# Filler products and a ScalarE softmax in the last attention steps of a gated graph network

## The chip, the cores and the metric

The kernel runs on one NeuronCore of a Trainium2 chip. The core has TensorE (matrix products, PE in the profile, with its weight loads as PEld), VectorE (DVE), ScalarE (ACT), GpSimd (POOL) and SyncE (SP), which starts the transfers. Each engine works through its own list of instructions in the order in which the program has them; engines wait for each other by semaphores. The metric is the device time of one execution in microseconds, the median of several runs. For the kernel before it is 2128.97 us (three runs, 2126.75 to 2130.69). The profile is one further execution, with a span of 2129.0 us from first to last instruction.

## The reference

There are 128 graphs of 128 nodes with 256 features, in float32. Layer 0 normalises and runs three rounds of a gated graph network; layer 1 is one attention step over each graph's edges. Cut to what is computed:

```python
# layer 0
h = relu(layernorm(x))
for i in range(3):
    m = h @ weight[i]
    aggr = einsum('bst,bsd->btd', A, m)          # A = adj != 0
    h = gru_cell(aggr, h, w_ih, w_hh, b_ih, b_hh)
x = x + h
# layer 1
h = relu(layernorm(x))
Wh = h @ W
s = Wh.sum(-1)
e = leaky_relu(s[:, :, None] + s[:, None, :], 0.2)
e = where(adj == 0, -inf, e)
x = x + softmax(e) @ Wh
```

## The kernel before

**Tiling.** The 128 graphs are cut into 32 groups of four (`G = 4`, `NG = 32`). A group goes through three gated rounds, `gru` for the first two and `gru_rows` for the third (which leaves the result with nodes on partitions in `x1`), and then through `attention`. The gate products of a round are fixed chains of float32 products into six banks of the accumulator memory (`x_rz`, `x_n`, `y_rz`, `y_n`, `q_rz`, `q_n`); two more banks, `misc`, serve everything else. The list `turns` says in which order the rounds of the groups take the gate banks, so that rounds of three groups lie interleaved. At the end groups 29, 30 and 31 remain, and the last entry is round 2 of group 31.

**What sets the order.** No engine's order is written out by hand. Every piece of work is recorded with `op(engine, ns, fn, reads, writes, ...)`: its engine, a price in ns, what it reads and writes, and a due time. `Plan.run` then lists all of them. It walks a model clock for each engine, takes of the pieces that are ready the one that can start first, and among equals the one with the lowest rank; the rank is the due time less all that must follow. Gate products are bound to a fixed order among themselves. Only the order that comes out goes into the program; the prices do not. An engine whose next instruction waits, waits, even where the one behind it could start. A buffer of kind `turn`, such as the gate banks, goes to its users in the order of their `phase`.

**The attention step.** Group 31 does it in two halves of two graphs (`lo`, `hi`), the others in one piece. For a group of four:

- `normed` (L488 to L504): statistics of `x1` on VectorE (`st`, `mv`), the reciprocal root on GpSimd (`rs`), `nm` on VectorE, and the normalised `h1` on ScalarE. There is one `h1` buffer, so the next group's waits until this group's products have read it.
- L899: four sums on VectorE give `s`; L917 puts the mask into `e`.
- L923: TensorE turns `s` into a row (`misc`); L929 and L930 add both on VectorE, L932 is the leaky slope, L934 the row maximum `top`, L936 `low`, the bias of the exponential.
- L941: ScalarE computes the exponentials; L943 and L944 their sums `den` and the reciprocals `rden`, on VectorE.
- For the last two groups TensorE turns `e` (L953) and ScalarE copies it to `eT` (L955); earlier groups do this by a transfer. L619 multiplies with `h1` in two halves `k`, each copied to `uT` by ScalarE (L624).
- L966 multiplies with the layer's weights ("rows product" in what follows, two graphs at a time), L971 scales by `rden` and adds to `x1` on VectorE, L974 stores.

Ahead of everything, L309 multiplies the identity `ident` (128 x 128, float32) with itself eight times[...].

Of the kernel before, what the change touches and what calls it, by code (L numbers as in the profile page):

```python
# [13 lines left out]
OP = mybir.AluOpType  # L14
# [5 lines left out]
ALPHA = 0.2  # L20
SETS = 4
EARLY = 3
SLOT = 18150
MARGIN = 8000
GATES = 18150
# [11 lines left out]
class Plan:  # L37
# [25 lines left out]
        uses.append(b)  # L63
        return b

    def op(self, eng, ns, fn, reads=(), writes=(), room=(), due=None, mark=None,
           turn=None, two=False, lag=None):

        i, deps = len(self.nodes), set()
        for b in room:
            if b.prev is not None:
                deps.update(a[0] for a in b.prev.accesses)
        for is_write, group in ((False, reads), (True, writes)):
            for item in group:
                b, lo, hi = item if isinstance(item, tuple) else (item, 0, 1 << 30)
                for j, w, l, h in b.accesses:
                    if (w or is_write) and l < hi and lo < h:  # L80
                        deps.add(j)
                if is_write and b.prev is not None:
                    deps.update(a[0] for a in b.prev.accesses)
        for is_write, group in ((False, reads), (True, writes)):
            for item in group:
                b, lo, hi = item if isinstance(item, tuple) else (item, 0, 1 << 30)
                b.accesses.append((i, is_write, lo, hi))
        deps.discard(i)
        bufs = {id(x[0] if isinstance(x, tuple) else x): (x[0] if isinstance(x, tuple) else x)
                for x in list(reads) + list(writes) + list(room)}  # L90
        free = [b for b in bufs.values() if self.tags[b.tag][1] in ("free", "turn")]
        for b in free:
            b.users.append(i)
            b.left += 1
        self.nodes.append([eng, ns, fn, deps, free, self.due if due is None else due,
                           two or eng == "POOL", self.LAG[eng] if lag is None else lag])
        if due is not None:
            self.chain.append(i)
        if mark is not None:
            self.marks[mark] = i  # L100
        if turn is not None:
            self.turns.append((i, turn))
# [108 lines left out]
def kernel(  # L211
# [79 lines left out]
    def ap(b):  # L291
        return phys[(b.tag,) + b.slot]
# [187 lines left out]
        to_sbuf("ACT", D, ps, W["w1_sum"], 0)  # L480


    def normed(src, dst, lo=0, hi=G):

        st, mv, rs, nm = buf("st"), buf("mv"), buf("rs"), buf("nm")
        part = slice(lo, hi)
        for b in range(lo, hi):
            op("DVE", 415, lambda b=b: nc.vector.bn_stats(ap(st)[:, b, :], ap(src)[:, b, :]),  # L488
               [(src, b, b + 1)], [(st, b, b + 1)])

        def aggr():
            for b in range(lo, hi):
                nc.vector.bn_aggr(ap(mv)[:, b, :], ap(st)[:, b, :])
        op("DVE", 160 * (hi - lo), aggr, [st], [mv])

        def rstd():
            nc.gpsimd.tensor_tensor(ap(rs)[:, part], ap(mv)[:, part, 1], eps[:, part], OP.add)
            nc.gpsimd.tensor_tensor(ap(rs)[:, part], ap(rs)[:, part], neghalf[:, part], OP.pow)
        op("POOL", 1300, rstd, [mv], [rs])
        op("DVE", 170, lambda: nc.vector.scalar_tensor_tensor(  # L500
            ap(nm)[:, part], ap(mv)[:, part, 0], -1.0, ap(rs)[:, part], op0=OP.mult, op1=OP.mult),
           [mv, rs], [nm])
        for b in range(lo, hi):
            op("ACT", 520, lambda b=b: nc.scalar.activation(  # L504
                ap(dst)[:, b, :], ap(src)[:, b, :], AF.Relu, bias=ap(nm)[:, b:b + 1],
                scale=ap(rs)[:, b:b + 1]), [(src, b, b + 1), rs, nm], [(dst, b, b + 1)])
# [384 lines left out]
    def attention(g, a, x1, h1, lo, hi):  # L891

        part, n = slice(lo, hi), hi - lo
        w1, w1_sum = W["w1"], W["w1_sum"]
        normed(x1, h1, lo, hi)
        s = buf("s")
        for b in range(lo, hi):
            hw = buf("hw")
            op("DVE", 520, lambda b=b, hw=hw: nc.vector.scalar_tensor_tensor(  # L899
                ap(hw), ap(h1)[:, b, :], 1.0, ap(w1_sum), op0=OP.mult, op1=OP.mult,  # L900
                accum_out=ap(s)[:, b:b + 1]), [(h1, b, b + 1), w1_sum], [hw, (s, b, b + 1)],
               two=True)

        e, top, low, den, rden = (buf(t) for t in ("e", "top", "low", "den", "rden"))

        def wide(t):
            return ap(t)[:, part, None].to_broadcast([P, n, N])

        def es():
            return ap(e)[:, part]

        def small(t):
            return ap(t)[:, part]
        cost = 155 + 134 * n
        op("DVE", 150 + 66 * n, lambda: nc.vector.tensor_scalar(  # L917
            es(), ap(a)[:, part], 0.0, -BIG, op0=OP.is_equal, op1=OP.mult), [(a, lo, hi)], [e])
        s_all = buf("misc")

        def turn_s():
            for b in range(lo, hi):
                nc.tensor.transpose(flat(s_all)[:, b * N:(b + 1) * N],  # L923
                                    ap(s)[:, b:b + 1].to_broadcast([P, P]), ident)

        def spread():
            return flat(s_all)[:, lo * N:hi * N].rearrange("p (b n) -> p b n", n=N)
        op("PE", 110 * n, turn_s, [s], [s_all], [e])
        op("DVE", cost, lambda: nc.vector.tensor_tensor(es(), es(), spread(), OP.add), [s_all], [e])  # L929
        op("DVE", cost, lambda: nc.vector.tensor_tensor(es(), es(), wide(s), OP.add), [s], [e],  # L930
           two=True)
        op("DVE", cost, lambda: nc.vector.scalar_tensor_tensor(  # L932
            es(), es(), ALPHA, es(), op0=OP.mult, op1=OP.max), [], [e], two=True)
        op("DVE", cost, lambda: nc.vector.tensor_reduce(small(top), es(), AX.X, OP.max),  # L934
           [e], [top])
        op("DVE", 150, lambda: nc.vector.tensor_scalar(  # L936
            small(low), small(top), -BIG / 1e3, -1.0, op0=OP.max, op1=OP.mult), [top], [low])

        def exps():
            for b in range(lo, hi):  # L940
                nc.scalar.activation(ap(e)[:, b, :], ap(e)[:, b, :], AF.Exp, bias=ap(low)[:, b:b + 1])  # L941
        op("ACT", 320 * n, exps, [low], [e], turn=(g + 2, 1, "rz"))
        op("DVE", cost, lambda: nc.vector.tensor_reduce(small(den), es(), AX.X, OP.add), [e], [den])  # L943
        op("DVE", 170, lambda: nc.vector.reciprocal(small(rden), small(den)), [den], [rden])  # L944
        eT, uT = buf("eT"), buf("uT")
        if g < NG - 2:
            turned_weights(e, eT)
        else:
            p_e = buf("misc")

            def turn():
                for b in range(lo, hi):
                    nc.tensor.transpose(flat(p_e)[:, b * N:(b + 1) * N], ap(e)[:, b, :], ident)  # L953
            op("PE", 110 * n, turn, [e], [p_e], [eT])
            op("ACT", 190 + 100 * n, lambda: nc.scalar.copy(  # L955
                ap(eT)[:, part].rearrange("p b n -> p (b n)"), flat(p_e)[:, lo * N:hi * N]),
               [p_e], [(eT, lo, hi)])

        weighted(h1, eT, uT, lo, hi)
        for m in range(lo, hi, 2):  # L960
            ps = buf("misc")

            def rows_product(m=m, ps=ps):
                for b in range(2):
                    for k in range(KD):
                        nc.tensor.matmul(ap(ps)[:, b, :], ap(uT)[:, k, (m + b) * N:(m + b + 1) * N],  # L966
                                         ap(w1)[:, k, :], start=(k == 0), stop=(k == KD - 1))
            op("PE", 4 * 432, rows_product,
               [(uT, m // 2, m // 2 + 1), (uT, 2 + m // 2, 3 + m // 2), w1], [ps])
            for b in range(2):  # L970
                op("DVE", 480, lambda b=b, i=m + b, ps=ps: nc.vector.scalar_tensor_tensor(  # L971
                    ap(x1)[:, i, :], ap(ps)[:, b, :], ap(rden)[:, i:i + 1], ap(x1)[:, i, :],
                    op0=OP.mult, op1=OP.add), [ps, rden], [(x1, m + b, m + b + 1)])
        op("SP", 100, lambda: nc.sync.dma_start(  # L974
            out[g * G + lo:g * G + hi].rearrange("b n d -> n b d"), ap(x1)[:, part]),
           [(x1, lo, hi)], [])
# [49 lines left out]
```

## Time and profile before

| what | value |
|---|---|
| time, median of 3 | 2128.97 us |
| span of the profiled run | 2129.0 us, mean granted TensorE clock 0.994 |
| TensorE busy | 2108.4 us |
| VectorE busy | 1701.3 us |
| ScalarE busy | 1536.5 us |
| GpSimd busy | 923.8 us |
| last gate product leaves TensorE | 2090.67 us |
| last rows product (L966) leaves TensorE | 2124.94 us |

A row of the profile's groups or of its list in order of time has the line in the code, the engine, the operation, `out<-in` by the names of the buffers, the shape, and how many instructions of this kind follow each other (`x8`); the start and the duration in us stand ahead of it in the list in order of time. A note in brackets gives the idle time before it and what ended it. A float32 product of the code can be more than one row of the trace. Matmuls are pipelined, so the recorded duration of one is longer than the distance to the next; for what a product costs, take the distance. The granted clock says at which share of its full clock TensorE was let run in a stretch.

### The profile page before, as it was taken

What the parts mean: (1) busy time and instruction counts of PE and PEld (TensorE: products, weight loads), DVE (VectorE), ACT (ScalarE), POOL (GpSimd) and SP (SyncE); (2) the same over time, 40 slices, a digit from 0 to 9 for tenths busy, and PEclk for the clock granted to TensorE, in tenths of its full rate; (3) what the DMA queues carried; (4) which work ended last, traced back from release to release, by engine and by line L of the source; (5) the groups of instructions that cost most, each with busy time, mean ns of one, the idle gap of its engine ahead of it and who ended that gap; (6) DMA issues with size and microseconds to landing.
All of it is one profiled execution on the core that took longest, in us unless ns stands there. A gap on an engine that the chain in (4) does not pass through costs nothing. (4 is left out here: it accounts for less than half of the span.)

```text
span 2129.0 us, 34073 instructions
## 1 busy us (share of the span) xinstructions
PE 2108.4 (99%) x12550; PEld 1882.8 (88%) x12550; DVE 1701.3 (80%) x3364; ACT 1536.5 (72%) x2771; POOL 923.8 (43%) x889
## 2 busy tenths in 40 slices
PE   8999999999999999999999999999999999999997
PEld 7888888898888998889998898998889988898896
DVE  7767898778787887877888787887878887877785
ACT  5567787767777676877767777677776777676663
POOL 5544454344543435434444443444434454434331
PEclk9999999999999999999999999999999999999997
DMA  4222223232222322323222322222223222212220
GB/s 144 45 50 50 48 51 72 50 65 54 64 67 55 79 56 50 68 58 80 45 60 58 75 67 50 65 56 64 66 55 75 60 50 70 60 31 53 58 75 30
DMA packets 333430, 129.35 MB, mean 61 GB/s; under 512 B 264656, under 2 KB 333008, under 8 KB 333264
## 3 DMA queue, kind: packets, MB, share of 16 engines
q1 hardware_dynamic: 333264, 127.18, 26.3%
q8 instruction: 98, 1.61, 0.3%
q14 instruction: 68, 0.56, 0.1%
HBM read 45.36 MB, written 16.78 MB: 29 GB/s over the span
## 5 line engine op out<-in xcount | busy, mean ns | idle before, releaser
L702 ACT COPY t_rz<-y_rz 128x512 f32<-128x512 f32 x192 | 112.3, 585 | 188.8 <-PE y_rz L663 114.3
L565 POOL TENSOR_TENSOR r<-rows 128x512 f32<-128x512 f32 x128 | 140.4, 1117 | 229.8 <-ACT rows L548 99.9
L712 DVE TENSOR_TENSOR t_rz<-t_rz,q_rz 128x512 f32<-128x512 f32 x192 | 131.3, 684 | 88.0 <-PE q_rz L663 40.4
L633 POOL TENSOR_TENSOR hs<-hT 128x512 f32<-128x512 f32 x96 | 131.8, 1373 | 156.3 <-PE y_n L670 72.4
L663 PE MATMUL y_rz<-hs,s_hh 128*128 128x256 f32 x768 | 197.4, 379 | 0.3 <-ACT t_rz L702 0.3
L663 PE MATMUL y_rz<-gs,s_x 128*128 128x256 f32 x768 | 197.1, 379 | 0.0
L663 PEld LDWEIGHTS y_rz<-gs,s_x 128*128 128x128 f32 x768 | 145.9, 190 | 19.8
L637 POOL TENSOR_TENSOR hs<-hT,hs 128x256 f32<-128x256 f32 x96 | 77.0, 802 | 198.1 <-PE q_n L670 160.4
L663 PEld LDWEIGHTS y_rz<-hs,s_hh 128*128 128x128 f32 x768 | 144.0, 190 | 20.1 <-issue 1.0
L590 POOL TENSOR_TENSOR pl<-d,pl 128x512 bf16<-128x512 f32 x64 | 80.8, 1264 | 185.1 <-ACT pl L588 184.9
L568 POOL TENSOR_TENSOR p<-r 128x512 bf16<-128x512 f32 x128 | 159.6, 1267 | 0.0
L712 DVE TENSOR_TENSOR t_n<-t_n,q_n 128x512 f32<-128x512 f32 x192 | 131.3, 684 | 26.4 <-PE q_n L670 12.6
L585 POOL TENSOR_TENSOR d<-hT,pl 128x512 f32<-128x512 f32 x64 | 77.6, 1214 | 139.2 <-DVE hT L791 65.2
L608 ACT COPY aT<-misc 128x512 f32<-128x512 f32 x192 | 112.0, 585 | 27.1 <-PE misc L605 23.3
L663 PE MATMUL x_rz<-hT,s_hh 128*128 128x256 f32 x512 | 131.5, 379 | 0.0
L663 PE MATMUL x_rz<-aT,s_x 128*128 128x256 f32 x512 | 131.4, 379 | 0.0
L966 PE MATMUL misc<-w,uT 128*128 128x256 f32 x512 | 125.5, 390 | 0.8 <-ACT uT L624 0.7
L829 POOL TENSOR_TENSOR x<-x,u 128x512 f32<-128x512 f32 x64 | 82.5, 1305 | 100.1 <-DMA x<-in_x_dram 54.9
L785 DVE TENSOR_TENSOR d<-hT,u 128x512 f32<-128x512 f32 x128 | 115.4, 901 | 10.5 <-ACT u L782 10.5
L663 PE MATMUL y_n<-hs,s_hh 128*128 128x256 f32 x384 | 114.3, 379 | 0.0
L663 PE MATMUL y_n<-gs,s_x 128*128 128x256 f32 x384 | 114.3, 379 | 0.0
L966 PEld LDWEIGHTS misc<-w,uT 128*128 128x128 f32 x512 | 98.6, 196 | 15.6 <-ACT uT L624 2.1
(219 smaller groups left out, 6418.5 us busy)
## 6 DMA issues: line engine op xcount, KB each, us to landing
rows<-in_x_dram SPq DMA_DIRECT2D x32, 512.0 KB, 4.2
x<-in_x_dram SPq DMA_DIRECT2D x32, 512.0 KB, 4.0
out_dram<-x SPq DMA_DIRECT2D x31, 512.0 KB, 2.9
at<-in_adj_dram SPq DMA_DIRECT2D x32, 256.0 KB, 2.8
plT<-pl SPq DMA_TRANSPOSE x186, 3.3
rz<-in_L_gnn_w_ih_dram SPq DMA_DIRECT2D x1, 768.0 KB, 5.0
rz<-in_L_gnn_w_hh_dram SPq DMA_DIRECT2D x1, 768.0 KB, 7.7
e<-in_L_gnn_weight_dram SPq DMA_DIRECT2D x3, 256.0 KB, 7.8
```

What stands on the lines that cost most here:

```text
L565: op("POOL", 1106, lambda part=part: nc.gpsimd.tensor_tensor(ap(r1)[:, part], ap(rows)[:, part], top(rows)[:, part], OP.subtract), [(rows, ...
L568: op("POOL", 1050, lambda part=part: nc.gpsimd.tensor_tensor(ap(p3)[:, part], ap(r1)[:, part], top(r1)[:, part], OP.subtract), [(r1, n, n ...
L585: op("POOL", 1150, lambda k=k, r=r: nc.gpsimd.tensor_tensor(ap(r), ap(hT)[:, k], part(pl, k, 0), OP.subtract), [(hT, 2 * k, 2 * k + 2), (p ...
L590: op("POOL", 1150, lambda k=k, r=r: nc.gpsimd.tensor_tensor(part(pl, k, 2), ap(r), part(pl, k, 1), OP.subtract), [r], [(pl, k, k + 1)])
L608: op("ACT", 590, lambda k=k, ps=ps: nc.scalar.copy(ap(dst)[:, k, :], flat(ps)), [ps], [(dst, 2 * k, 2 * k + 2)])
L633: op(eng, cost, lambda: sub(ap(w)[:, 0:2, :], blocks()[:, 1::2, :], blocks()[:, 0:2, :], OP.subtract), [t], [(w, 0, 2)], two=True)
L663: nc.tensor.matmul(ap(bank)[:, half, :], ap(w)[:, i - 1, q, :], source(t, sums), start=(first and c == 0 and m == 0), stop=False, skip_gro ...
L702: op("ACT", 590, lambda: nc.scalar.copy(ap(t), ap(y)), [y], [t], mark=mark)
L712: op("DVE", 690, lambda: nc.vector.tensor_tensor(ap(t), ap(t), ap(q), OP.add), [q], [t])
L785: op("DVE", 690, lambda j=j, d=d, cols=cols: nc.vector.tensor_tensor(ap(d), ap(hT)[:, j, :], ap(u)[:, cols], OP.subtract), [(hT, lo, hi), ...
L829: op("POOL", 1290, lambda cols=cols, part=part: nc.gpsimd.tensor_tensor(part(x1), part(x1), ap(u)[:, cols], OP.add), [(u, lo, hi)], [(x1, ...
L966: nc.tensor.matmul(ap(ps)[:, b, :], ap(uT)[:, k, (m + b) * N:(m + b + 1) * N], ap(w1)[:, k, :], start=(k == 0), stop=(k == KD - 1))
```

## The change

It has two parts, both at the end of the run.

The first adds filler products on TensorE in the attention steps of groups 30 and 31. `warm(t, ns)` records a piece of TensorE work that reads `t` (so that it can't stand before `t` is there), multiplies a slice of `t` with the identity and then the identity with itself `ns // 110` times. All of it goes into the bank `x_n`, as a use of that bank after the last gates, and nothing reads the result. The pieces carry `late=True`, a due time behind all other work. They are for TensorE's clock, so that it stays up in the stretches in which TensorE waits for the softmax.

The second applies to groups 29, 30 and 31 (`ENDING = 3`). The addition of `s` and the leaky slope (L930 and L932) become one ScalarE instruction per graph, a Prelu with `s` as its bias, and the sums of the exponentials (L943) become the accumulator output of the exponentials themselves. This is for VectorE, which is then free of three operations per group.

The line numbers of the changed kernel are higher: L619 becomes L650, L923 becomes L956, L941 becomes L984, L953 becomes L999, L966 becomes L1012 and L971 becomes L1017; the fillers are L500 (the read of `t`) and L502 (identity with identity).

```diff
+ENDING = 3
...
     def op(self, eng, ns, fn, reads=(), writes=(), room=(), due=None, mark=None, late=False,
            turn=None, two=False, lag=None):
...
-        self.nodes.append([eng, ns, fn, deps, free, self.due if due is None else due,
+        self.nodes.append([eng, ns, fn, deps, free, 10 ** 9 if late else self.due if due is None else due,
                            two or eng == "POOL", self.LAG[eng] if lag is None else lag])
...
+    def warm(t, ns, get=None):
+        if plan.group < NG - 2:
+            return
+        if not after_gates:
+            phase_now, plan.phase = plan.phase, len(turns)
+            after_gates.append(buf("x_n"))
+            plan.phase = phase_now
+        b = after_gates[0]
+
+        def products():
+            here = flat(b)
+            what = get() if get else plain(t)[:, :P]
+            cols = what.shape[1]
+            nc.tensor.matmul(here[:, :cols], ident, what, start=False, stop=False, skip_group_check=True)
+            for _ in range(ns // 110):
+                nc.tensor.matmul(here[:, :P], ident, ident, start=False, stop=False,
+                                 skip_group_check=True)
+        op("PE", 60 + ns, products, [t, b], [], late=True)
...
     def normed(src, dst, lo=0, hi=G):
...
+            if dst is not src:
+                warm((st, b, b + 1), 330, lambda b=b: ap(st)[:, b, :])
...
+        if dst is not src:
+            warm(mv, 1100, lambda: ap(mv)[:, lo, :])
...
+        if dst is not src:
+            warm(nm, 440, lambda: ap(nm)[:, part])
...
     def attention(g, a, x1, h1, lo, hi):
...
+        ending = g >= NG - ENDING
...
+            warm((h1, b, b + 1), 440, lambda b=b: ap(h1)[:, b, :P])
...
-        op("DVE", cost, lambda: nc.vector.tensor_tensor(es(), es(), wide(s), OP.add), [s], [e],
-           two=True)
-        op("DVE", cost, lambda: nc.vector.scalar_tensor_tensor(
-            es(), es(), ALPHA, es(), op0=OP.mult, op1=OP.max), [], [e], two=True)
+        def leaky():
+            for b in range(lo, hi):
+                nc.scalar.activation(ap(e)[:, b, :], ap(e)[:, b, :], AF.Prelu, bias=ap(s)[:, b:b + 1],
+                                     alpha=ALPHA)
+        if ending:
+            op("ACT", 320 * n, leaky, [s], [e])
+        else:
+            ...
...
+        warm(top, 110, lambda: small(top))
...
+        warm(low, 330 * n, lambda: small(low))
...
                 nc.scalar.activation(ap(e)[:, b, :], ap(e)[:, b, :], AF.Exp, bias=ap(low)[:, b:b + 1],
+                                     **(dict(accum_out=ap(den)[:, b:b + 1]) if ending else {}))
-        op("ACT", 320 * n, exps, [low], [e], turn=(g + 2, 1, "rz"))
-        op("DVE", cost, lambda: nc.vector.tensor_reduce(small(den), es(), AX.X, OP.add), [e], [den])
+        op("ACT", (400 if ending else 320) * n, exps, [low],
+           [e, den] if ending else [e], turn=(g + 2, 1, "rz"))
+        if not ending:
+            op("DVE", cost, lambda: nc.vector.tensor_reduce(small(den), es(), AX.X, OP.add), [e], [den])
```

More of the change, by code (lines that the diff above doesn't have):

```diff
@@ L64, in buf, with op @@
         return b
-    def op(self, eng, ns, fn, reads=(), writes=(), room=(), due=None, mark=None,
+    def op(self, eng, ns, fn, reads=(), writes=(), room=(), due=None, mark=None, late=False,
            turn=None, two=False, lag=None):
@@ L480, in weights @@
         to_sbuf("ACT", D, ps, W["w1_sum"], 0)
+    def warm(t, ns, get=None):
[15 more added lines that the diff above has]
+        op("PE", 60 + ns, products, [t, b], [], late=True)
+    after_gates = []
     def normed(src, dst, lo=0, hi=G):
@@ L929, in attention @@
         op("DVE", cost, lambda: nc.vector.tensor_tensor(es(), es(), spread(), OP.add), [s_all], [e])
-        op("DVE", cost, lambda: nc.vector.tensor_tensor(es(), es(), wide(s), OP.add), [s], [e],
-           two=True)
-        op("DVE", cost, lambda: nc.vector.scalar_tensor_tensor(
-            es(), es(), ALPHA, es(), op0=OP.mult, op1=OP.max), [], [e], two=True)
+        def leaky():
[5 more added lines that the diff above has]
+        else:
+            op("DVE", cost, lambda: nc.vector.tensor_tensor(es(), es(), wide(s), OP.add), [s], [e],
+               two=True)
+            op("DVE", cost, lambda: nc.vector.scalar_tensor_tensor(
+                es(), es(), ALPHA, es(), op0=OP.mult, op1=OP.max), [], [e], two=True)
         op("DVE", cost, lambda: nc.vector.tensor_reduce(small(top), es(), AX.X, OP.max),
            [e], [top])
+        warm(top, 110, lambda: small(top))
         op("DVE", 150, lambda: nc.vector.tensor_scalar(
             small(low), small(top), -BIG / 1e3, -1.0, op0=OP.max, op1=OP.mult), [top], [low])
+        warm(low, 330 * n, lambda: small(low))
         def exps():
             for b in range(lo, hi):
-                nc.scalar.activation(ap(e)[:, b, :], ap(e)[:, b, :], AF.Exp, bias=ap(low)[:, b:b + 1])
-        op("ACT", 320 * n, exps, [low], [e], turn=(g + 2, 1, "rz"))
-        op("DVE", cost, lambda: nc.vector.tensor_reduce(small(den), es(), AX.X, OP.add), [e], [den])
+                nc.scalar.activation(ap(e)[:, b, :], ap(e)[:, b, :], AF.Exp, bias=ap(low)[:, b:b + 1],
+                                     **(dict(accum_out=ap(den)[:, b:b + 1]) if ending else {}))
[3 more added lines that the diff above has]
+            op("DVE", cost, lambda: nc.vector.tensor_reduce(small(den), es(), AX.X, OP.add), [e], [den])
         op("DVE", 170, lambda: nc.vector.reciprocal(small(rden), small(den)), [den], [rden])
```

## The prediction

> **What bounds the kernel now.** I read the page's busy shares first, then TensorE by windows of time, then its waits, then the chain that ended last, and last the list in order of time from 2070 us on.
>
> From the busy shares: TensorE is the wall, and no other engine is near it.
>
> ```profile
> PE 2108.4 (99%) x12550; PEld 1882.8 (88%) x12550; DVE 1701.3 (80%) x3364; ACT 1536.5 (72%) x2771; POOL 923.8 (43%) x889
> ```
>
> TensorE's waits from 60 to 2090 us sum to 2.2 us. So the body cannot gain more than 2.2 us, and whatever the change wins or loses comes after 2090.67 us, where the last gate product leaves the array. The same engine by windows there (columns: stretch, length, busy time of PE, weight loads, DVE, ACT, POOL, granted clock, DMA):
>
> ```profile
> 2093.50:2096.90 3.40, 0.90 (x5) 0.45 (x3) 3.40 (x7) 1.36 (x4) 1.57 (x1) 0.98 0.00 0
> 2096.90:2100.30 3.40, 2.57 (x11) 2.20 (x12) 3.30 (x8) 1.13 (x3) 0.00 (x0) 0.50 0.00 0
> ...
> 2107.10:2110.55 3.45, 3.45 (x10) 2.71 (x9) 1.65 (x6) 0.00 (x0) 0.00 (x0) 0.52 0.00 0
> 2110.55:2113.90 3.35, 1.15 (x7) 0.56 (x5) 2.48 (x7) 0.36 (x2) 0.00 (x0) 0.99 0.00 0
> 2113.90:2117.30 3.40, 2.85 (x11) 2.44 (x12) 2.77 (x9) 1.67 (x6) 0.00 (x0) 0.50 0.16 57
> ```
>
> The clock column halves after a stretch with 0.90 us of TensorE work, and returns after one that is full. This is what the fillers are for. What the halving costs is seen in the list in order of time, with the same eight products at full and at half clock:
>
> ```profile
> 2078.07 1.06 PE L619 MATMUL misc<-eT,h 128*128 128x128 f32 x8
> 2090.78 3.62 PE L966 MATMUL misc<-w,uT 128*128 128x256 f32 x16
> 2098.82 2.08 PE L619 MATMUL misc<-eT,h 128*128 128x128 f32 x8 [0.68 <-ACT eT L955]
> 2104.32 6.72 PE L966 MATMUL misc<-w,uT 128*128 128x256 f32 x16 [0.68 <-ACT uT L624]
> ```
>
> The chain that ended last shows the end: TensorE's last products, two adds, the store.
>
> ```profile
> 2117.76 3.42 PE misc L966 x8
> ...
> 2123.36 1.58 PE misc L966 x6
> 2124.94 0.02 issue
> 2124.97 0.48 DVE x L971
> ```
>
> Last, the price of a filler. A filler is a float32 product of the identity with itself, and the kernel already has eight of exactly this form at its start (L309, two loops of four). The trace has 16 rows for them:
>
> ```profile
> L309 PE MATMUL y_rz<-ident x8: 421/421/581, 1.4 to 3.0; 128*128 128x128 f32 x8
> L309 PE MATMUL y_n<-ident x8: 274/421/421, 3.2 to 4.6; 128*128 128x128 f32 x8
> ```
>
> So each `matmul(ident, ident)` in the code is two products in the trace. A transpose (L923, L953) is one row for one.
>
> [...]0.50 and 1.00 alternate at about 2096.9, 2110.5, 2113.9 and 2120.7 us, all multiples of 3.4 us apart, and 2.57 us busy of 3.40 were not enough to return. [...]a 128-column float32 product takes two rows of 0.111 us (L619: 8 rows from 2077.97 to 2078.86 us of weight loads), one in bf16 (L605) starts every 0.055 us, so 0.222 against 0.055. [...]the trace has one load, of 1.28 us, for Tanh, Exp, Relu and copies together.
>
> **The change part by part.** The new order of instructions on each engine is the built program's own; it is fixed, and an engine takes its list from the top.
>
> *Slope and sums on ScalarE, groups 29 to 31.* Removes from VectorE L930, L932 and L943: 3 x 0.69 us for a group of four graphs, 3 x 0.42 for each half of the last group. Adds to ScalarE one Prelu per graph, nearest row L941 (0.32 us apart in a row of four), and an accumulator on Exp; before has no such row, so between 0.08 us (VectorE's accumulator read in L899)[...]; I take the first. Prelu could need another table set: [...]I take 0, since five functions share the one load. Neither end matters: ScalarE is 9.60 us busy in the 34.27 us from 2090.67 to 2124.94 us, and the walk below leaves it waiting for TensorE. Value on the path: 0.
>
> *Fillers.* They may write only `x_n`'s bank, in a phase after the last gates, so all of them stand behind the last gate product: none delays a gate. But from there they stand between the real products. The planner prices a filler at 110 ns (`ns // 110`); it takes 0.222 us at full clock. The planner put them where it saw holes of its own size, and TensorE cannot skip them. Walking TensorE's new list from 2090.67 us (t = 0), at full clock:
>
> ```
>  t end  what stands there
>   4.4   4 x (h1 read + 4 fillers), 1.11 each
>   7.9   group 29 rows product, 16 rows x 0.2206   (before: at 0 to 3.5)
>  10.7   low + 12 fillers (2.8)
>  11.2   group 30 transposes, 4 x 0.135; operand ready about 7.5
>  13.9   top + 1 filler, mv + 10 fillers
>  18.0   sums k=0 (0.89), mv + 10 fillers (2.35), sums k=1 (0.89)
>  23.5   mv + 10, 2 x (nm + 4), h1 + 4
>  25.8   turn_s, rows product (1.75), turn_s
>  29.0   h1 + 4, nm + 4, h1 + 4
>  31.1   rows product, transposes (31 a)
>  34.9   2 x (low + 6), sums 31 a (0.89)
>  38.7   h1 + 4, transposes (31 b), st + 3, rows product
>  44.5   sums 31 b in two parts, 3 x and 3 x (st or mv's source + 3)
>  46.2   last rows product
> ```
>
> Check by sum. Real work: 48 rows of 256 columns x 0.2206 (3.53 / 16) = 10.6; 32 rows of 128 x 0.111 = 3.55; 12 transposes x 0.135 (L923, 0.54 / 4) = 1.6; together 15.75 us. Fillers ahead of the last rows product: 120 x 0.222 = 26.6. Reads of `h1` (8 x 0.222) = 1.8. Reads of 2 to 6 columns, 17 of them: two rows each of a weight load and almost no columns; before shows none, so between half a product, 0.11, and a whole one, 0.222, that is 1.9 to 3.8; I take 0.13 since the columns nearly vanish: 2.2. Sum 46.4 us, and TensorE ends at 2090.67 + 46.4 = 2137.1 instead of 2124.94 us: **12.1 us later**. In this walk every operand is ready before TensorE arrives, by 1.6 us at the tightest (the first part of group 31 waits for `eT` and `uT` copies, ready at 35.4 against a need at 37.0). So TensorE never idles, the clock stays full, and nothing of the fillers is hidden.
>
> *What the fillers win.* At full clock the real products are 15.75 us instead of the 26.19 us busy that the trace has for the stretch: 10.4 us. TensorE's idle time, 34.27 - 26.19 = 8.1 us, goes too. Together 18.5 us are freed and 30.6 us are put in: the same +12.1.
>
> *What follows.* VectorE's two adds and the store keep their 4.06 us from 2124.94 to 2129.00. Fillers behind the last rows product (5 of them and three small reads, 1.5 us) end inside these 4 us: nothing.
>
> *The body.* The changed ends move the planner's ranks, and the lists differ from some 230 rows down VectorE's on. The work and the chain of gates are the same, so TensorE's sum is; the new order can save at most the 2.2 us, and may cost some. I take 0.
>
> Total: 2129.0 + 12.1 = 2141.1, so **2141 us**, slower by 0.57%.
>
> **The rivals.**
> 1. *The fillers cost what the planner says* (0.11 us, one row each). For it: its prices for other products fit, 225 ns for a 128-column one, 110 for a transpose. Against: L309 shows two rows each. Then 15.75 + 128 x 0.111 + 2.2 = 32.2 us, less than 34.27; with 0 to 4 us of waits the kernel ends between 2127 and 2131, say 2128: not slower. Chance 0.06.
> 2. *The body stalls in its new order.* For it: the order is another almost everywhere, and TensorE is at 99%. Against: the old one had only 2.2 us of waits by the same planner. Stalls of 4 to 8 us on top: 2145 to 2149, say 2147. Chance 0.12.
> 3. *The clock falls all the same*, because products of 4 columns or of the identity don't hold it. For it: 2.57 us busy of 3.40 did not raise it. Against: L619's form at the same density sits inside the gates at 1.00, and the fillers are of its shape. If half the stretch runs at half clock: + 23 us, 2164. Chance 0.03.
>
> **How the numbers follow.** My forecast has 0.79: 2141. Its own width: reads 1.9 to 3.8 instead of 2.2 (-0.3 to +1.6); [...]a few waits or stalls (+2). With rival 2 mostly inside, the range is 2135 to 2148. Faster by over 0.2% (under 2124.7): 0.03, a third or so of rival 1 and a body that gains. Within 0.2%: 0.05. Slower: 0.92.
>
> **What would show it.** TensorE's busy time after the last gate near 46 us with no idle time, and clock 1.00 in every window up to its last product; filler groups with two rows per product, 0.11 us apart; the transposes of group 30 behind 12 fillers, with ScalarE's `eT` copy waiting for TensorE; last rows product near 2137 us; the body ending within 2 us of 2090.7. It is wrong if fillers show one row each, if TensorE idles between them, if the clock is 0.50 anywhere after 2091 us, or if the last gate product moves by more than 4 us.

## The result, and the profile after

The changed kernel takes 2142.78 us (median of four runs, 2142.75 to 2142.78) against 2129.24 us before (median of four): the ratio is 1.0065, with a 95% interval of 1.0047 to 1.0082. It is slower, as forecast (2141), and the profiled span went from 2129.0 to 2140.9 us. A span is 2 to 3 us shorter than the time of the same execution, which was 2142.75 us for the changed kernel and 2131.72 us for before, more than its median.

The busy shares of the changed kernel, first line of its page:

```profile
PE 2131.5 (100%) x12856; PEld 1910.4 (89%) x12856; DVE 1702.6 (80%) x3352; ACT 1541.9 (72%) x2795; POOL 932.4 (44%) x889
```

TensorE is 23.1 us busier than before (2108.4), for a span that is 11.9 us longer. Its windows after the last gate (columns as before: stretch, length, busy PE, weight loads, DVE, ACT, POOL, granted clock, DMA) show the rest:

```profile
2093.40:2096.80 3.40, 3.40 (x19) 3.01 (x18) 1.37 (x3) 1.28 (x8) 0.00 (x0) 1.00 0.00 0
2096.80:2100.20 3.40, 3.40 (x32) 3.37 (x31) 3.30 (x9) 0.00 (x0) 0.42 (x1) 1.00 0.02 5
...
2110.40:2113.80 3.40, 3.40 (x31) 3.37 (x31) 0.14 (x1) 0.00 (x0) 0.00 (x0) 1.00 0.03 5
...
2134.20:2137.60 3.40, 3.40 (x27) 3.19 (x25) 0.74 (x2) 0.00 (x0) 0.00 (x0) 1.00 0.00 0
```

Where the old kernel had windows with 0.90, 2.57 and 1.15 us of TensorE work, and a clock that fell to 0.50 twice, the new one has 3.40 us of 3.40 and a clock of 1.00. The fillers did what they are for. But in the window at 2110.4 VectorE has 0.14 us of work and ScalarE none: the softmax now stands and waits for TensorE. The list in order of time of the same kernel, TensorE alone, shows behind what:

```profile
2093.49 3.62 PE L1012 MATMUL misc<-w,uT 128*128 128x256 f32 x16
2096.95 0.28 PE L500 MATMUL x_n<-low,ident 128*128 128x4 f32 x2
2097.09 2.92 PE L502 MATMUL x_n<-ident 128*128 128x128 f32 x24
2099.85 0.60 PE L999 MATMUL misc<-ident,e 128*128 128x128 f32 x4
2100.29 0.28 PE L500 MATMUL x_n<-top,ident 128*128 128x4 f32 x2
2100.43 0.47 PE L502 MATMUL x_n<-ident 128*128 128x128 f32 x2
2100.74 0.28 PE L500 MATMUL x_n<-mv,ident 128*128 128x2 f32 x2
2100.88 2.48 PE L502 MATMUL x_n<-ident 128*128 128x128 f32 x20
2103.19 1.06 PE L650 MATMUL misc<-eT,h 128*128 128x128 f32 x8
...
2134.93 1.89 PE L1012 MATMUL misc<-w,uT 128*128 128x256 f32 x8
```

The transposes of group 30 (L999) start at 2099.85 behind 12 fillers, which are 24 rows. Their operand was there at 2094.7 us, when the last exponential ended. Until 2096.95 us the rows product of group 29 held TensorE; the 2.9 us after that are the read of `low` and the fillers. The waits from 2089 us on name the engines that pay (who waits and for whom: us in total, how often, the longest):

```profile
DVE x L1017 <- PE misc L1012: 20.5, 5, 7.2
ACT uT L655 <- PE misc L650: 11.9, 4, 3.2
...
ACT eT L1001 <- PE misc L999: 9.1, 3, 5.8
```

TensorE itself waits for nobody after the last gate. VectorE kept to its list while it waited: it stood 3.7 us for L956, until 2113.66 us, and the sum behind it (L932), whose `h1` ScalarE had finished at 2109.97 us, started at 2114.00 us. In what follows "the tail" is the time from the start of the first weight load behind the last gate product to the end of the last rows product: 34.3 us before (2090.67 to 2124.93) and 47.9 us after (2088.92 to 2136.82).

### The profile page after: what moved, and what is told of

It is laid out like the page before. It is cut to its first block, busy times and chain, and to the rows that moved or that the text cites. A ratio compares the mean times of both kernels' runs of the same rounds, so it can differ in the third digit from the quotient of the medians.

```text
span 2140.9 us, 34711 instructions
## 1 busy us (share of the span) xinstructions
PE 2131.5 (100%) x12856; PEld 1910.4 (89%) x12856; DVE 1702.6 (80%) x3352; ACT 1541.9 (72%) x2795; POOL 932.4 (44%) x889
## 4 chain that ended last, share of the span: by engine, by line
PE 98%; DVE 1%; DMA 1%; ACT 0%; issue 0%; SPq 0%; DVEq 0%
PE y_rz L694 15%; PE x_rz L694 10%; PE q_rz L694 10%; PE y_rz L701 8%; PE y_n L694 8%; PE misc L636 6%; PE q_rz L701 5%; PE misc L1012 5%; PE x_n L694 5%; PE x_rz L701 5%; PE q_n L694 5%; PE y_n L701 4%; PE q_n L701 3%; PE x_n L701 3%; PE misc L650 3%; PE x_n L502 1%
## 5 line engine op out<-in xcount | busy, mean ns | idle before, releaser
L743 DVE TENSOR_TENSOR t_n<-t_n,q_n 128x512 f32<-128x512 f32 x192 | 131.1, 683 | 25.1 <-PE q_n L701 11.3
L639 ACT COPY aT<-misc 128x512 f32<-128x512 f32 x192 | 112.1, 585 | 27.5 <-PE misc L636 23.1
L1012 PE MATMUL misc<-w,uT 128*128 128x256 f32 x512 | 120.5, 379 | 0.0
L664 DVE TENSOR_TENSOR gs<-aT 128x512 f32<-128x512 f32 x96 | 89.3, 931 | 26.7 <-ACT aT L639 26.6
```

What stands on the lines that cost most here:

```text
L639: op("ACT", 590, lambda k=k, ps=ps: nc.scalar.copy(ap(dst)[:, k, :], flat(ps)), [ps], [(dst, 2 * k, 2 * k + 2)])
L664: op(eng, cost, lambda: sub(ap(w)[:, 0:2, :], blocks()[:, 1::2, :], blocks()[:, 0:2, :], OP.subtract), [t], [(w, 0, 2)], two=True)
L743: op("DVE", 690, lambda: nc.vector.tensor_tensor(ap(t), ap(t), ap(q), OP.add), [q], [t])
```

## The experiments

Each ratio is to the kernel before, run on the same chip, with its 95% interval. A tail is that of the one profiled run. The edits of the first five runs and of the true price are to the changed kernel; the others build on a run with bfloat16 fillers, and are shown against it.

**The ScalarE part alone.** `warm` returns at once.

```diff
     def warm(t, ns, get=None):
-        if plan.group < NG - 2:
-            return
+        return
```

> The fillers left out, the ScalarE part kept. Theory A (the loss is TensorE's time for the fillers, 0.222 us each at full clock, and ScalarE's part lies beside it): without them the half-clock stretch is back and the time is near before's; the new order's body ends 1.8 us earlier as in the changed kernel, and the exponentials of group 30 start about 1.4 us sooner after it: 2125 to 2128 us. Rival B (ScalarE's part costs too: the accumulator reads and the Prelu lengthen the softmax): over 2131 us.

Measured: 2127.69 us, ratio 0.9990 (0.9983 to 0.9997); the tail is 32.4 us. So ScalarE's part does not cost, it wins 1.7 us between the medians, though its accumulator is not free: the trace of the changed kernel has 12 reads of 0.19 us. Rival B falls. The half clock is back, as the windows show:

```profile
2098.80:2102.20 3.40, 2.35 (x12) 2.05 (x13) 3.37 (x10) 0.91 (x2) 1.09 (x2) 0.67 0.00 0
2102.20:2105.60 3.40, 2.73 (x10) 2.16 (x9) 2.06 (x12) 2.14 (x5) 1.26 (x3) 0.50 0.45 154
```

One thing of the expectation was wrong: the body did not end earlier. In this run, with the body order of the changed kernel, it ended at 2092.36 us (the profiled run was the slowest of the 21); in others of the same order at 2090.09 and 2090.26.

**The fillers alone.** Slope and sums stay on VectorE; apart from fillers, the order on TensorE is that of before.

```diff
-ENDING = 3
+ENDING = 0
```

> The fillers kept, the ScalarE part left out; the order up to the last gate is then that of before. Theory A: all 129 fillers stand ahead of the last rows product here; real work 15.75 + 129 x 0.222 + 8 reads x 0.222 + 20 small reads x 0.23 = 50.8 us after the last gate product at 2090.7, then 4.1 us: 2145 to 2146 us, with TensorE at full clock. Rival B (ScalarE's part bears a share of the loss): under 2139 us.

Measured: 2148.37 us (2145.94 to 2149.87), ratio 1.0085 (1.0071 to 1.0098), above the forecast by 2 us. The tail is 49.7 us. The 129 fillers of the expectation were a miscount: there are 125, and with these the sum is 15.75 + 27.75 + 1.8 + 4.6 = 49.9 us. In this order all fillers stand ahead of the last rows product, as the end of TensorE's list shows:

```profile
2138.18 0.28 PE L500 MATMUL x_n<-top,ident 128*128 128x2 f32 x2
2138.33 0.47 PE L502 MATMUL x_n<-ident 128*128 128x128 f32 x2
2138.63 1.89 PE L1012 MATMUL misc<-w,uT 128*128 128x256 f32 x8
```

Together with the run before, this puts the whole loss on the fillers.

**Half as many fillers**, at the same places of the same order.

```diff
-            for _ in range(ns // 110):
+            for _ in range(ns // 220):
```

> The changed kernel in its own order, with half as many fillers in each piece (ns // 220), so that a piece takes what the planner charges. Theory A: 56 fillers instead of 120 ahead of the last rows product, 15.75 + 56 x 0.222 + 1.8 + 3.9 = 33.8 us after 2088.9, then 4.1: 2127 us, up to 2130 with waits; TensorE has idle time again. Rival C (the loss comes from the order, from real products that stand behind a piece whose operand is late): at least 2136 us.

Measured: 2129.66 us, ratio 1.0002 (0.9994 to 1.0010), tail 33.6 us against 33.8 worked out. With one and the same order the loss goes from 13.5 us to nothing by the number of products alone. Rival C (the order makes the loss) falls. One detail was wrong: TensorE still had no idle time, it was the wall to the end.

**Fillers in bfloat16**, same order, same number.

```diff
+    ident16 = const.tile([P, P], BF16, name="ident16")
+    nc.vector.tensor_copy(ident16, ident)
...
-                nc.tensor.matmul(here[:, :P], ident, ident, start=False, stop=False,
+                nc.tensor.matmul(here[:, :P], ident16, ident16, start=False, stop=False,
```

> The changed kernel in its own order and with its own number of fillers, but each a bfloat16 product of the identity with itself ([...]0.055 us instead of 0.222). Theory A: 15.75 + 120 x 0.055 + 1.8 + 3.9 = 28 us of TensorE work after 2088.9 leaves room, and the chain of the softmax at full clock sets the end: 2120 to 2125 us. Rival C (order): at least 2136 us. Rival D (shorter fillers do not hold the clock): half clock in the last 30 us and about 2128 to 2132 us.

Measured: 2123.42 us, ratio 0.9971 (0.9959 to 0.9982), tail 27.8 us. The list in order of time, TensorE, shows 12 fillers as 12 rows, and the transposes of group 30 behind them 0.8 us after the read of `low` (2.9 us in the changed kernel):

```profile
2092.31 3.67 PE L1014 MATMUL misc<-w,uT 128*128 128x256 f32 x16
2095.82 0.28 PE L502 MATMUL x_n<-low,ident 128*128 128x4 f32 x2
2095.96 0.83 PE L504 MATMUL x_n<-ident 128*128 128x128 bf16 x12
2096.63 0.61 PE L1001 MATMUL misc<-ident,e 128*128 128x128 f32 x4
```

The clock was 1.00 to the end of the tail, so rival D falls too, and the kernel is faster than before.

**Fillers as transposes.** Same order, same number; the transpose of the identity is one row in the trace.

```diff
-                nc.tensor.matmul(here[:, :P], ident, ident, start=False, stop=False,
-                                 skip_group_check=True)
+                nc.tensor.transpose(here[:, :P], ident, ident)
```

> The changed kernel in its own order and with its own number of fillers, but each a float32 transpose of the identity, one row in the trace for one in the code, which is what the planner charges (110 ns). Theory A (the loss is the second row of each filler): 15.75 + 120 x 0.111 to 0.135 + 1.8 + 3.9 = 34.8 to 37.7 us after the last gate product, then 4.1: 2129 to 2132 us with the clock full. Rival D (transposes do not hold the clock): half clock after 2095 us, so that real work and fillers are slower: over 2138 us.

Measured: 2129.72 us, ratio 1.0003 (0.9994 to 1.0011), tail 33.4 us, clock 1.00 in every window of the tail. The group row gives one row for each of 125 fillers:

```profile
L502 PE MATMUL x_n<-ident 128*128 128x128 f32 x125 | 18.7, 278 | 0.0
```

This is the kernel in which a filler takes what the planner charges, 0.11 us (a read of `h1` and four fillers take 0.66 us here, 1.11 in the changed kernel). It ends about where the kernel with half the products ends: 125 instructions of one row cost about what 57 of two rows do (114 rows). Among these float32 rows of 0.11 us the number of rows counted, not that of instructions; a bfloat16 row took half as long (0.056 us: 12 in 0.67 us, from 2095.96 to 2096.63 us in the kernel with bfloat16 fillers).

**Reads in bfloat16 as well**, by the upper halves of the float32 numbers; same order.

```diff
+            what = what.bitcast(BF16)
+            what = what[:, 1::2]
...
-            nc.tensor.matmul(here[:, :cols], ident, what, start=False, stop=False, skip_group_check=True)
+            nc.tensor.matmul(here[:, :cols], ident16, what, start=False, stop=False, skip_group_check=True)
```

> As the kernel with bfloat16 fillers, same order, and now the reads of the operand in bfloat16 too (the upper halves of its float32 numbers[...]). Theory A: in the last run TensorE still had no idle time, so its sum still sets the end; 25 reads get cheaper by 8 x 0.17 + 17 x 0.17 = 4.2 us: 2119 us, up to 2121 where waits of the softmax come in. Rival (the softmax chain at full clock already sets the end with bfloat16 fillers): no change, 2123 us.

Measured: 2121.29 us, ratio 0.9967 (0.9955 to 0.9980), tail 25.3 us, 2.4 less than with bfloat16 fillers alone, instead of the 4.2 worked out. TensorE begins to wait here, and the list of waits shows only little of it:

```profile
PE misc L960 <- DVE hw L936: 0.2, 1, 0.2
PE x_n L504 <- DVE mv L524: 0.2, 1, 0.2
```

Short waits vanish behind recorded durations that overlap: the four transposes of group 30 take 0.56 us from their start to the start of what follows (2095.45 to 2096.01), against 0.44 us with bfloat16 fillers alone (2096.63 to 2097.07). Where the whole rest of the 1.8 us went is not shown.

**The planner charging half** for the same bfloat16 products, which changes their places.

```diff
-        op("PE", 60 + ns, products, [t, b], [], late=True)
+        op("PE", 60 + ns // 2, products, [t, b], [], late=True)
```

> The same products, and the planner charges half (60 + ns // 2), which is what they take, so that it places them by their true length, all of them ahead of the last rows products' wait. Theory A: the sum is as in the kernel with bfloat16 reads, 2118 to 2122 us. Rival C (order matters by itself): differs from that kernel by more than 3 us.

Measured: 2121.39 us, ratio 0.9967 (0.9954 to 0.9979), tail 25.8 us. Another order, the same time.

**Half of the bfloat16 fillers**, with bfloat16 reads, in the changed kernel's order (`ns // 220`).

> The kernel with bfloat16 fillers and reads in the changed kernel's order, with half as many fillers (ns // 220). Theory A: TensorE's sum falls by 64 x 0.055 = 3.5 us to about 20 us after the last gate, below what the softmax chain takes, so TensorE waits and the end is the chain's at full clock, 2116 to 2120 us; if the clock falls again[...], 2121 to 2127 us.

Measured: 2120.78 us (2120.14 to 2122.24), ratio 0.9962 (0.9950 to 0.9975): the lowest median of all, 0.38% under the kernel before, though the two kernels ahead of it (2121.29 and 2121.39) lie within the scatter. The tail is 24.9 us; the clock is 1.00 throughout the tail, and the list of waits has 1.7 us for TensorE. The fillers taken out were to save 3.5 us of its work, and the tail is 0.4 us shorter: the amount of fillers no longer sets the end.

**No products of the identity**, bfloat16 reads alone.

```diff
-            for _ in range(ns // 220):
+            for _ in range(0):
```

> The kernel with bfloat16 reads, with no products of the identity left: 25 reads of 0.055 us or less are all that stands between the real products. It tells how little holds the clock. With half the fillers the emptiest window had 2.81 us of 3.40 busy and stayed at full clock; without any the window between group 29's rows product and the transposes of group 30 falls to about 2.2. If that is enough: 2119 to 2121 us, as with half. If the clock falls as it did without reads and fillers: half clock from about 2099 us on and 2124 to 2128 us.

Measured: 2122.34 us, ratio 0.9969 (0.9957 to 0.9980), between the two expectations: the clock fell, but within the tail for one window only. The windows are set here on the edges at which the clock changes:

```profile
2096.04:2099.46 3.42, 2.26 (x17) 1.82 (x18) 3.39 (x10) 1.17 (x2) 0.95 (x2) 1.00 0.00 0
2099.46:2102.87 3.41, 2.02 (x14) 1.31 (x13) 2.83 (x14) 2.35 (x5) 1.28 (x3) 1.00 0.32 110
2102.87:2106.28 3.41, 3.27 (x12) 2.38 (x10) 1.62 (x8) 0.90 (x3) 0.00 (x0) 0.50 0.13 44
```

The window with 2.02 us of work is followed by one at half clock; that one was nearly full (3.27 us), and the clock came back. The difference to half the fillers, 1.6 us in different sets of runs, is near the scatter.

**The true price, float32 fillers**, all of them.

```diff
-        op("PE", 60 + ns, products, [t, b], [], late=True)
+        op("PE", 230 + 2 * ns, products, [t, b], [], late=True)
```

> The changed kernel's float32 fillers, all of them, with the planner charging their true length (230 + 2 x ns); it now puts 15 of the pieces behind the last rows product. Theory A in its plain form (the amount is what costs, wherever it stands): all 129 fillers and 28 reads still run before the kernel can end, 15.75 + 28.6 + 1.8 + 4.6 = 50.8 us after 2090.3: 2141 to 2144 us, now ending with the fillers and not with the store. Rival E (the wrong price alone made the loss, and a right one mends it): 2130 us or less.

Measured: 2142.62 us, ratio 1.0066 (1.0052 to 1.0079), the same as the changed kernel. The last rows products are out earlier, but the fillers run on behind them:

```profile
2122.71 3.62 PE L1012 MATMUL misc<-w,uT 128*128 128x256 f32 x16
...
2139.34 0.28 PE L500 MATMUL x_n<-top,ident 128*128 128x2 f32 x2
2139.48 0.47 PE L502 MATMUL x_n<-ident 128*128 128x128 f32 x2
```

TensorE is done at 2139.95 us, 49.7 us after the last gate: the same as with the fillers alone, and again the sum for 125 fillers. So the wrong price is not by itself the cause (rival E falls). The amount is.

**Half of the bfloat16 fillers without the ScalarE part** (`ENDING = 0` again).

> The kernel with half the bfloat16 fillers, without the ScalarE part (slope and sums on VectorE again). With TensorE no longer the wall the softmax chain binds, so ScalarE's part should now be worth what it took off that chain: at half clock, without fillers, it was 1 to 2 us. Theory A: 2122 to 2124 us. Rival: no difference, 2120 to 2121 us.

Measured: 2126.20 us (2124.80 to 2129.77), ratio 0.9987 (0.9980 to 0.9993), tail 28.2 us against 24.9 with the ScalarE part. So with TensorE out of the way that part seems to be worth more than I expected: about 3.3 us of tail, 5.4 us between the two medians, which come from different sets of runs. The order of the fillers differs as well, so not all of it need be ScalarE's.

## Why the prediction was right

The step that decided was right: a filler is two rows and takes 0.222 us (eight rows take 0.89 us, from 2089.25 to 2090.14 us), twice its price. The trace of the changed kernel has 250 rows for the 125 of them that it records, 0.275 us of recorded time each where they start 0.111 us apart:

```profile
L502 PE MATMUL x_n<-ident x250: 275/275/356, 2089.3 to 2138.3; 128*128 128x128 f32 x125
```

The other steps, in their order:

- *ScalarE's part, 0 on the path.* Right for the changed kernel, where ScalarE waits for TensorE. Where TensorE is not the wall it wins: 1.7 us without fillers. That Prelu would bring no table load of its own was an estimate; the trace of the changed kernel has one load, of 1.28 us, as before. The accumulator is a row of 0.19 us, where the 0.08 taken was an estimate from VectorE's accumulator read (L899, 0.080 to 0.084 us), but it overlaps with the next instruction: exponentials of group 30 start 0.38 to 0.40 us apart instead of 0.29 to 0.31, so it costs about 0.09 us each, near that estimate.
- *The walk.* Its times from the last gate, against the trace with the first filler read (2089.03 us) as zero: what follows the transposes of group 30 begins at 11.2, in the trace at 11.3; the first turn of `s` of group 31 begins at 23.5, in the trace at 24.2; the last rows product is out at 46.2, in the trace at 47.8. No wait of TensorE in either.
- *The small reads* were mis-sized. I took 0.13 us, and they take 0.23, the upper bound: an `nm` read and four fillers take 1.12 us from one start to the next (2109.89 to 2111.01), and 4 x 0.222 of it are fillers. For 17 of them this is 1.7 us more. The sum of 46.4 becomes 48.1, measured 47.9; the 48 rows of the rows products went 0.216 us apart instead of 0.2206, which is the 0.2 us that remains.
- *The body, 0.* In the profiled run it ended 1.8 us earlier, which hid the reads in the span: by luck the span came out at 2140.9 us, beside the 2141.1 worked out. Of this 0.8 us lies in the first 30 us (TensorE busy 24.51 us instead of 23.73), where both kernels have the same list, and 0.6 us between 60 and 2060 us; the rest I did not trace. It is scatter more than order: the runs with this body order ended it between 2088.9 and 2092.4 us. The start differs from run to run, also in its clock: from 12 to 18 us it is 0.79 in the changed kernel and full without fillers, from 24 to 30 us it is full in the first and 0.84 in the second.
- *What follows, 4.06 us.* In the trace 2136.82 to 2140.9: 4.1.
- *Rival 2 (stalls in the body)*: 1.6 us of waits instead of 2.2. *Rival 3 (the clock falls all the same)*: 1.00 in every window up to 2137.6 us. Before, the clock fell after a window with 1.03 us of TensorE work (2093.37 to 2096.78 us), and the last section has windows with up to 2.02. *Rival 1 (one row each)* did not happen, but its number, 2128, is about what the two kernels with half the rows gave (2129.7 each).

The predicted loss of 12.1 us lies within the interval of the measured one (13.5 us, 10.0 to 17.5); the spans alone differ by 11.9. The low end of the predicted range, 2135 us, was my estimate, with no figure of a trace behind it. That the total of 2141 us is so near the measured time has some luck too. The prediction added the loss to the span of before, 2129.0 us, and compared the sum with times, which are longer; but the profiled run of before took 2.5 us more than the median (2131.72 against 2129.24), so that its span happened to be about the median time.

## What to carry to other kernels

Price filler work by the rows that the trace shows for its data type, from an instruction of the same form that already runs, and add it all up. Together with TensorE's own real work it must stay below the length of the chain that it is to accompany, whatever a scheduler's prices say. Keeping the clock up was worth having here, and a thin filler was enough: half of the bfloat16 fillers, with bfloat16 reads and the ScalarE part, turned a loss of 0.65% into a gain of 0.38%. Take the upper bound for float32 products of few columns: in the trace of the changed kernel each of their two rows has a weight load of 128 columns ahead of it (0.19 us of recorded time), and they cost as much as full ones (0.23 us against 0.222). That the load is the reason was not tested.

## What the runs showed of the hardware

- A float32 product with 2 to 6 columns took about 0.23 us in the changed kernel, as much as one with 128 (0.222 us): `low`, 4 columns, and 12 fillers took 2.90 us from start to start (2096.95 to 2099.85), an `st` read, 6 columns, and three fillers 0.89 us (2129.13 to 2130.02). In bfloat16 the read of `low` and 12 fillers took 0.69 us together (2094.76 to 2095.45 us in the kernel with bfloat16 reads); at 0.056 us for a filler that leaves about 0.02 us for the read, an estimate.
- With transposes as the only fillers, between reads and real products, the clock was 1.00 in every window from 2088 to 2126 us. The transposes are 18.7 us of recorded time there, and TensorE is 37.3 us busy. What part of the clock is owed to them was not separated.
- The clock fell after windows in which TensorE still had work. In the trace of before it changes at 2096.78, 2110.44, 2113.85 and 2120.67 us, 13.66, 3.41 and 6.82 us apart; so the windows here are 3.41 us long and set on edges at which it changes. It fell after 1.03 us (before), 1.85 us (without fillers) and 2.02 us (reads only) of recorded TensorE time; in the run with reads only it held after 2.26 us. It came back after 3.27 us (reads only), and did not after 2.81 (before). No one amount of recorded time divides the cases. The first pair of windows is from the run without fillers, where the clock fell after 1.85 us; the second is from the run with half the bfloat16 fillers and without the ScalarE part, where it held after 1.86 us, and fell only after the empty window:

```profile
2096.53:2099.94 3.41, 1.85 (x10) 1.31 (x11) 3.31 (x8) 2.18 (x9) 0.00 (x0) 1.00 0.00 0
2099.94:2103.36 3.42, 2.72 (x12) 2.13 (x10) 3.35 (x13) 0.59 (x1) 1.93 (x4) 0.50 0.00 0
...
2117.29:2120.70 3.41, 1.86 (x8) 1.09 (x7) 0.88 (x2) 0.25 (x1) 0.00 (x0) 1.00 0.21 73
2120.70:2124.12 3.42, 0.00 (x0) 0.00 (x0) 0.00 (x0) 0.00 (x0) 0.00 (x0) 1.00 0.23 77
```
